# More warm-up matmuls ahead of the first products, and an early silu on ScalarE, in a two-layer adaptive FFN kernel

## The chip, the cores and the metric

The kernel runs on one core of a Trainium2 chip. The metric is the device time of one execution in microseconds; lower is better. A core has a matrix engine (TensorE, PE in the profile, with its weight loads shown as PEld), a vector engine (VectorE, DVE), a scalar engine (ScalarE, ACT), GpSimd (POOL) and SyncE (SP), which here issues DMA transfers. Each engine works through its own queue in order and waits on semaphores of the others.

## The reference

For x of 8 x 128 tokens with 512 features, two layers are computed, each as x + FFN(condition(x)).

```python
# layer 0
base = x @ W.T
logits = x @ Wr.T + 5.0 * one_hot(language_id)         # 8 experts
gates = softmax over the two largest logits, else 0
c = base + 2.0 * sum_e gates[e] * (x @ A[e].T) @ B[e].T  # rank 16
w_gu, w_d = dequant(4-bit weights, zeros, scales by group)
gate, up = split(c @ w_gu)                               # 1376 each
x = x + (silu(gate) * up) @ w_d
# layer 1
c = x @ weight[adapter_id].T                             # one of 8 per sequence
n = c * rsqrt(mean(c**2) + 1e-5) * ln_w
x = x + (silu(n @ gate_w.T) * (n @ up_w.T)) @ down_w.T   # 1792 inner
```

## The kernel before, in words

All activations lie transposed, features on the 128 partitions and tokens on the free axis, in two blocks of 512 tokens (`TB`). A float32 product that must be precise is made of three products of split operands (high part, low part, difference), with a rescale of the sum in PSUM between them.

The part that the change touches is the beginning, `network_in` and in it `by_groups_of_scales`. From `written_order()` on, the order of instructions on TensorE, VectorE, ScalarE and GpSimd is the order of the program text.

- L362 loads the router and low-rank weights `wa`, the eight x blocks `xb` of 128 tokens (block 0 in two halves from ScalarE's queue, blocks 1 to 7 from SP's), then the base weights `wT` and `bT`. They arrive in that order.
- L386 to L389: a tile of ones is set by VectorE, and TensorE multiplies it by itself `NWARM` times into a PSUM tile named `idle`, which nobody reads.
- L854: a one-element Exp on ScalarE into `root`, a cell of the tile `line`.
- `experts` (L436): for each x block, four matmuls of 128 x 136 give the router logits and the low-rank rows; 64 in all.
- L502 to L526: ScalarE and VectorE split x and the base weights.
- `base_products` (L533) adds the products of the base; `rescale_base` (L547) rescales its sums on ScalarE between products of the parts; `gated` (L455 to L482) makes the gates, with an Exp at L468; `turned` (L553) transposes them; `low_rank` (L559) adds the low-rank part; `split_condition` (L824 on ScalarE, L825 on VectorE) splits the result into the tile `a`.
- `gate_up_pair` (products at L682, rescales at L313 and L315): two chunks of 128 gate and up columns at a time, for each of four groups of scales. A gate sum ends in a silu on ScalarE (L698, tile `sl`), an up sum in a product on VectorE (L701, tile `h`). The four PSUM pairs are reused by the next chunk pair in the same order, so its first gate product waits for the first silu, and its first up product for the first `h`.
- `down` (L732), then layer 1: adaptation (L1292), normalisation, gate and up products (L1480), down products (L1628), all in an order that a planner in the kernel writes out.

ScalarE keeps one table of functions loaded at a time. The program contains no instruction for that: the compiler puts one (ACT_TABLE_LOAD in the profile) ahead of an activation whose function the loaded table lacks.

Of the kernel before, what the change touches and what calls it, by code (L numbers as in the profile page):

```python
# [20 lines left out]
AF = mybir.ActivationFunctionType  # L21
# [4 lines left out]
NT = B * T  # L26
TB = 512
NTB = NT // TB
NWARM = 20
KC = D // P  # L30
E, R = 8, 16
LANG_BIAS = 5.0
# [189 lines left out]
def network_in(ctx, tc, a, out, by_groups, flag, again):  # L222
    nc = tc.nc
# [8 lines left out]
    def bank(name):  # L232
        return pair(name)[:, 0, :]
# [10 lines left out]
    root = line[:, :1]  # L244
# [142 lines left out]
    idle = bank("idle")[:, :P]  # L387
    for _ in range(NWARM):
        nc.tensor.matmul(idle, lhsT=ones, rhs=ones, start=True, stop=True)  # L389
# [8 lines left out]
    eps = const.tile([P, 1], F32, name="eps")  # L398
# [93 lines left out]
    def x_parts(tb, b=None):  # L492
        rows = slice(tb * TB, (tb + 1) * TB) if b is None else slice(b * T, (b + 1) * T)
        at = slice(0, TB) if b is None else slice((b * T) % TB, (b * T) % TB + T)
        return a3[0][:, :, rows], a3[1][:, :, rows], xd[tb][:, :, at]

    def rows(tb):
        return range(tb * (TB // T), (tb + 1) * (TB // T))
# [15 lines left out]
    def x_diff(tb):  # L514
        for b in rows(tb):
            hi, lo, di = x_parts(tb, b)
            nc.vector.tensor_tensor(di, hi.bitcast(F32), lo.bitcast(F32), ALU.subtract)
# [28 lines left out]
    def rescale_base(ps):  # L546
        nc.scalar.activation(ps, ps, AF.Copy, scale=HLSCALE)  # L547
# [48 lines left out]
    def by_groups_of_scales():  # L596
# [25 lines left out]
        def queue_zeros(j0, j1, name):  # L622
            w = CH0[j0]
            zq = gup.tile([P, 2 * KC, j1 - j0, w], U16, tag="zq", bufs=1, name="zq")
            for j in range(j0, j1):
                zqs[j] = zq[:, :, j - j0, :]
            for s in range(8):
                queue("dve", name, 0.1 + 0.06 * (j1 - j0), lambda s=s: zeros_gu(zq, qz, s, j0, j1))
# [258 lines left out]
        hg1 = gated(1, [kept[:, i].rearrange("p (b n) -> p b n", b=2) for i in range(2)])  # L887
        for ps in pairs1:
            rescale_base(ps)
        x_diff(1)  # L890
        queue_zeros(0, 4, "zeros")
        for j in range(4):
# [259 lines left out]
    if by_groups:  # L1152
        by_groups_of_scales()
    else:
        in_float32()
# [725 lines left out]
```

## Time and profile before

| | us |
|---|---|
| median of 3 runs (lowest, highest) | 415.1 (414.18, 416.61) |
| profiled execution, its own time | 415.66 |
| span of the profile, first to last instruction | 413.6 |
| PE busy | 405.8 |
| DVE busy | 368.1 |
| ACT busy | 304.2 |
| POOL busy | 29.7 |

Busy time is the sum of the stretches in which an engine had an instruction running. A row of the timeline gives the start, the time from that start to the last instruction's end, the engine, the line, the operation with output and input tiles, the shape, the number of instructions merged, and in brackets the idle time ahead of it with the one that ended it. A row of the wait list gives who waited, for whom, the total in us, how many times, and the longest.

Four ACT_TABLE_LOAD instructions stand in the profile: at L854, L698, L807 and L1407, of 1.28 us each.

### The profile page before, as it was taken

Reading aid. Unit: us, or ns where it says so; the run is one execution under the profiler, and the core shown is the slowest. Engines: PE = TensorE matmul, PEld = TensorE weight load, DVE = VectorE, ACT = ScalarE, POOL = GpSimd, SP = SyncE. Lnnn points to the kernel's source line nnn. Section 1 sums busy time; section 2 is a strip of 40 time slices with the busy share of each in tenths; the row PEclk is TensorE's granted clock in tenths of the full one; section 3 lists DMA queues with packets and bytes.
Section 4 is the critical chain, followed back from the end, with each engine's and each line's share of the span. In section 5 each row is a group of like instructions: output and inputs, shape, how many; then the busy total and the mean of one; then the engine's idle time right before and its main releaser. Section 6 shows DMA issues by size and latency. Waiting matters only on the chain.

```text
span 413.6 us, 5170 instructions
## 1 busy us (share of the span) xinstructions
PE 405.8 (98%) x1763; PEld 319.1 (77%) x1763; DVE 368.1 (89%) x678; ACT 304.2 (74%) x501; POOL 29.7 (7%) x35
## 2 busy tenths in 40 slices
PE   8999999999999999999999999999999999999995
PEld 8886778888888867445777888888888888888884
DVE  3998979997999788988999999989999899988973
ACT  5832688867986887387999888866976688767751
POOL 1000200000000400421011011011011101000000
PEclk9999999999999999999999999999999999999999
DMA  8930840110020450682144114323333225000005
GB/s 280 397 148 0 241 91 0 52 26 32 2 63 2 151 180 1 215 309 73 52 141 89 65 25 119 84 52 91 101 65 90 71 45 140 0 1 2 25 2 208
DMA packets 17041, 38.59 MB, mean 93 GB/s; under 512 B 1904, under 2 KB 8944, under 8 KB 15984
## 3 DMA queue, kind: packets, MB, share of 16 engines
q1 hardware_dynamic: 11472, 25.09, 18.6%
q0 software_dynamic: 5104, 12.72, 12.2%
q10 hardware_dynamic: 432, 0.39, 0.3%
q8 instruction: 15, 0.25, 0.3%
q14 instruction: 18, 0.15, 0.1%
HBM read 36.10 MB, written 2.10 MB: 92 GB/s over the span
## 4 chain that ended last, share of the span: by engine, by line
PE 89%; DVE 5%; ACT 2%; DMA 1%; issue 1%; SPq 0%; ACTq 0%; DVEq 0%
PE bank L1480 30%; PE bank L1628 18%; PE down L732 9%; PE gate L682 9%; PE up L682 8%; PE bank L1292 6%; PE base L533 5%; PE experts L436 2%; PE base L559 2%; DMA xb<-in_first 1%; DVE xt L1260 1%; DVE a L1257 1%; PE bank L1333 1%; DVE down L315 1%; ACT sl L698 1%
## 5 line engine op out<-in xcount | busy, mean ns | idle before, releaser
L1227 ACT ACTIVATE bank<-bank 128x512 f32<-128x512 f32 (+1 forms) x126 | 71.2, 581 | 23.5 <-PE bank L1480 14.0
L1628 PE MATMUL bank<-h,d 128*128 128x512 f32 (+1 forms) x249 | 67.3, 382 | 0.0
L1628 PEld LDWEIGHTS bank<-h,d 128*128 128x128 f32 x249 | 45.6, 188 | 9.2 <-DVE h L1105 0.2
L682 PE MATMUL gate<-a,dq 128*128 128x512 f32 (+1 forms) x176 | 47.9, 394 | 0.4 <-ACT sl L698 0.4
L682 PE MATMUL up<-a,dq 128*128 128x512 f32 (+1 forms) x176 | 47.5, 392 | 0.0
L1480 PE MATMUL bank<-a,w 128*128 128x512 f32 x168 | 45.2, 391 | 0.4 <-ACT snap L1227 0.4
L1480 PE MATMUL bank<-xs,w 128*128 128x512 f32 x168 | 44.3, 391 | 0.0
L732 PE MATMUL down<-h,wd 128*128 128x512 f32 (+1 forms) x176 | 41.7, 391 | 0.1
L682 PEld LDWEIGHTS gate<-a,dq 128*128 128x128 f32 (+1 forms) x176 | 32.4, 185 | 9.0 <-ACT sl L698 0.9
L732 PEld LDWEIGHTS down<-h,wd 128*128 128x128 f32 (+1 forms) x176 | 32.9, 188 | 7.9 <-DVE h L701 0.5
L682 PEld LDWEIGHTS up<-a,dq 128*128 128x128 f32 (+1 forms) x176 | 32.3, 185 | 8.0 <-DVE a L825 0.3
L1480 PEld LDWEIGHTS bank<-a,w 128*128 128x128 f32 x168 | 31.2, 188 | 7.8 <-ACT snap L1227 0.8
L313 ACT ACTIVATE gate<-gate,ratio 128x1024 f32<-128x1024 f32 (+1 forms) x26 | 28.2, 1085 | 11.6 <-PE gate L682 11.6
L1480 PEld LDWEIGHTS bank<-xs,w 128*128 128x128 f32 x168 | 31.4, 188 | 6.5
L1227 ACT ACTIVATE snap<-bank 128x512 f32<-128x512 f32 x42 | 25.0, 596 | 13.6 <-PE bank L1480 13.4
L1108 DVE SCALAR_TENSOR_TENSOR w<-w 128x512 fp32r<-128x512 f32 x50 | 34.1, 682 | 0.1
L1095 POOL DMA_DIRECT2D raw<-in_wgu x14 | 17.9, 1281 | 199.0 <-PE up L682 46.2
L1685 DVE SCALAR_TENSOR_TENSOR xT<-bank,xT 128x512 f32<-128x512 f32 (+1 forms) x41 | 27.4, 673 | 4.2 <-PE bank L1628 3.8
L1514 DVE SCALAR_TENSOR_TENSOR snap<-bank,snap 128x512 f32<-128x512 f32 x42 | 28.2, 684 | 2.2 <-PE bank L1480 2.0
L1628 PE MATMUL bank<-w,d 128*128 128x512 f32 x96 | 30.0, 389 | 0.0
L1292 PE MATMUL bank<-w,xT 128*128 128x512 f32 x64 | 28.9, 594 | 0.0
L1105 DVE TENSOR_TENSOR w<-raw,w 128x512 fp32r<-128x512 f32 x42 | 28.6, 682 | 0.2 <-ACT w L1102 0.2
(169 smaller groups left out, 740.0 us busy)
## 6 DMA issues: line engine op xcount, KB each, us to landing
raw<-in_wgu SPq DMA_DIRECT2D x13, 640.0 KB, 3.9
raw<-in_wgu POOLq DMA_DIRECT2D x14, 256.0 KB, 4.5
wd<-in_wd SPq DMA_DIRECT2D x14, 256.0 KB, 2.6
qw<-in_qw_gu SPq DMA_DIRECT2D x5, 512.0 KB, 5.2
xT<-in_xT SPq DMA_DIRECT2D x2, 1024.0 KB, 12.0
xb<-in_first SPq DMA_DIRECT2D x7, 256.0 KB, 4.9
out<-xT SPq DMA_DIRECT2D x5, 256.0 KB, 2.2
qwd<-in_qw_d SPq DMA_DIRECT2D x2, 512.0 KB, 9.0
```

Source lines behind the costliest of these rows:

```text
L313: nc.scalar.activation(ps, ps, AF.Copy, scale=by)
L533: nc.tensor.matmul(base[m], lhsT=wT3[i][:, m, c * P : (c + 1) * P], rhs=x_parts(tb)[i][:, c, :], start=(i == 0 and c == 0), stop=(i == 1 a ...
L682: nc.tensor.matmul(ps, lhsT=dqs[j][:, c, half, :], rhs=a3[i][:, c, tb * TB : (tb + 1) * TB], start=(c == 0 and i == 0), stop=(i == 1), ski ...
L732: nc.tensor.matmul(ps[:, tb], lhsT=wds[k][:n, m * P : (m + 1) * P], rhs=h2[k][i][:, tb], start=(first and i == 0), stop=(i == 1), skip_gro ...
L1105: nc.vector.tensor_tensor(lo, raw, hi.bitcast(F32), ALU.subtract)
L1108: nc.vector.scalar_tensor_tensor(di, lo.bitcast(F32), -1.0 / EPS, hi.bitcast(F32), ALU.mult, ALU.add)
L1227: nc.scalar.activation(out_, in_, AF.Copy, scale=by)
L1292: nc.tensor.matmul(of("bank", "ad", b), lhsT=xT[:, c, b * T : (b + 1) * T], rhs=of("w1", b)[:, c * D : (c + 1) * D], start=(c == 0), stop= ...
L1480: nc.tensor.matmul(ps, lhsT=w[:, i, n, c * P : (c + 1) * P], rhs=x[i][:, c0 + c], start=(first and i == which[0] and c == 0), stop=True, s ...
L1514: nc.vector.scalar_tensor_tensor(x, of("bank", j, bank_), by, x, ALU.mult, ALU.add)
L1628: nc.tensor.matmul(of("bank", *who)[:, : c1 - c0], lhsT=of("d", j)[:, i, m * P : (m + 1) * P], rhs=h_tile(j, tb)[:, i, c0:c1], start=((i, ...
L1685: nc.vector.scalar_tensor_tensor(x, ps, by_end, x, ALU.mult, ALU.add)
```

## The change

The number of warm-up matmuls on the tile of ones goes from 20 to 33. Behind the rescales of the second token block's base sums, ScalarE runs a one-element silu of `eps` into `root`, the cell that L854 and L807 also write. No other instruction is edited, added or moved by hand.

```diff
-NWARM = 20
+NWARM = 33
...
         for ps in pairs1:
             rescale_base(ps)
+        nc.scalar.activation(root, eps, AF.Silu)
         x_diff(1)
```

## The prediction

> **What bounds the kernel now.** I read the page first, for who is busy and which chain ends last.
>
> ```profile
> span 413.6 us, 5170 instructions
> PE 405.8 (98%) x1763; PEld 319.1 (77%) x1763; DVE 368.1 (89%) x678; ACT 304.2 (74%) x501; POOL 29.7 (7%) x35
> PE 89%; DVE 5%; ACT 2%; DMA 1%; issue 1%; SPq 0%; ACTq 0%; DVEq 0%
> ```
>
> TensorE is busy for 98% of the span and is 89% of the chain. Nearly every microsecond that it loses or wins is therefore carried to the end, and I need the few places where it isn't doing useful work at full pace. The list of what it waited for, TensorE alone, longest in total first:
>
> ```profile
> PE idle L389 <- DVE ones L386: 1.1, 1, 1.1
> PE gate L682 <- ACT sl L698: 0.4, 1, 0.4
> PE experts L436 <- DMA xb<-in_first: 0.4, 2, 0.2
> ```
>
> The second and third are what this change touches. Now the order of time, TensorE alone, in the first 13 us, from four windows: the start of the span, a pair of narrow ones in the second x block, and one late in the experts.
>
> ```profile
> 1.06 2.32 PE L389 MATMUL idle<-ones 128*128 128x128 bf16 x20 [1.06 <-DVE ones L386]
> 3.60 2.18 PE L436 MATMUL experts<-wa,xb 128*128 128x136 f32 x8 [0.23 <-DMA xb<-in_first]
> 5.95 7.52 PE L436 MATMUL experts<-wa,xb 128*128 128x136 f32 x56 [0.17 <-DMA xb<-in_first]
> 13.22 3.99 PE L533 MATMUL base<-a,wT 128*128 128x512 f32 x16
> ...
> 6.57 0.66 PE L436 MATMUL experts<-wa,xb 128*128 128x136 f32 x2
> 6.34 1.34 PE L436 MATMUL experts<-wa,xb 128*128 128x136 f32 x5
> 8.79 4.33 PE L436 MATMUL experts<-wa,xb 128*128 128x136 f32 x36
> ```
>
> Matmuls of a row overlap, so I take their spacing. Five of the same matmul take 0.68 us more than two, so early they stand (1.34 - 0.66) / 3 = 0.227 us apart. Late, 36 take 4.33 us, of which the last one's own 0.28 us is taken off: 4.05 / 35 = 0.116 us. The pace doubles somewhere between 7.2 us and 8.8 us. The column of the granted clock prints 1.00 throughout these windows, so the clock is read here from the pace. The twenty warm-ups stand (2.32 - 0.31) / 19 = 0.106 us apart (one lasts 0.31 us).
>
> Last, the end of the first gate/up pair, all engines, where ScalarE loads its table for silu:
>
> ```profile
> 55.12 1.08 ACT L313 ACTIVATE up<-up,ratio 128x1024 f32<-128x1024 f32 x1
> 56.22 1.28 ACT L698 ACT_TABLE_LOAD   x1
> 57.16 1.07 PE L682 MATMUL up<-a,dq 128*128 128x512 f32 x4
> 57.51 2.12 ACT L698 ACTIVATE sl<-gate,small 128x1024 f32<-128x1024 f32 x2
> 58.66 2.48 DVE L701 SCALAR_TENSOR_TENSOR h<-up,small,sl 128x1024 f32<-128x1024 f32 x2 [2.66 <-ACT sl L698]
> 58.68 1.20 PE L682 MATMUL gate<-a,dq 128*128 128x512 f32 x4 [0.45 <-ACT sl L698]
> 59.72 1.16 PE L682 MATMUL up<-a,dq 128*128 128x512 f32 x4
> ```
>
> ScalarE is ready at 56.20; the load takes until 57.50, the first silu ends near 58.63, and only then is the gate bank free for TensorE's next pair.
>
> **Part A: 33 warm-ups.** It adds 13 matmuls on TensorE at 0.106 us: 1.38 us at the slow pace. Behind them in TensorE's queue stands everything else. Cover: the twentieth is followed by a hole from 1.06 + 20 x 0.106 = 3.18 to 3.60 us (x block 0 is on its way), and block 0 by another to 5.95 us (block 1). With 33 the first expert starts at 1.06 + 33 x 0.106 = 4.56, and eight of them end at 4.56 + 8 x 0.227 = 6.38, against block 1's landing at 5.95. If the faster pace comes no sooner than now, the cost is 0.43 us at most; the restart that vanishes gives some back (the first matmul of block 1 stands 6.34 - 5.95 = 0.39 us before the second, where 0.227 is usual: 0.16), which leaves 0.27. That is one end.
>
> The other end: the faster pace is there before 5.95. Then the 56 matmuls take 56 x 0.116 = 6.50 us in place of 13.22 - 5.95 = 7.27, a gain of 0.77. It can't be more for this execution, since the landing at 5.95 stays.
>
> Which? The pace doubled some 3.9 us after TensorE started on experts at 3.60, through one hole of about 0.37 us, though warm-ups had run for 2.1 us before the hole at 3.18. If a stream without the first hole earns the pace in the same 3.9 us, 33 warm-ups earn it at 1.06 + 3.9 = 4.96, ahead of 5.95. So I stand near the gain: -0.6, a fifth less than the full 0.77 because a single execution can't show how much the moment varies.
>
> [...]
>
> Does the gain last? Other work stays in time: ScalarE's first weight split waits for wT at 10.53, and the base products would need it at 13.22 - 0.77 = 12.45; it ends at 11.16. From there to 58 us the wait list shows TensorE waiting for nobody, so it carries the gain along.
>
> **Part B: the silu behind the rescales.** It adds a table load (1.28 us in all four loads of the trace) and a 128x1 ACTIVATE (0.20 us at L854): 1.48 us on ScalarE, and takes the load out of L698. ScalarE there, alone:
>
> ```profile
> 28.93 1.01 ACT L547 ACTIVATE base<-base 128x1024 f32<-128x1024 f32 x1 [0.86 <-PE base L533]
> 34.29 1.02 ACT L824 ACTIVATE a<-base 128x1024 fp32r<-128x1024 f32 x1 [4.35 <-PE base L559]
> ```
>
> The next instruction, the split at L824, waits 4.35 us for TensorE. The added 1.48 us lies inside with 2.87 to spare: cost nothing. Without that cover it would delay the split by up to 1.48. The last Exp (L468, 25.80) is ahead, and what follows up to L698 are copies, which run between the silus of L698 today without a load. The added ACTIVATE writes a cell of its own and adds no DMA and no wait but for the memset of eps, done at 1.2 us.
>
> At L698 the first silu would then run from 56.22 to 57.34 and the second to 58.46. TensorE's groups of four stand 0.91 us apart, so it reaches the next gate group at 57.16 + 0.91 = 58.07, finds the bank free, and wins 58.68 - 58.07 = 0.61. The two groups after the stall, 1.20 and 1.16 us against 1.07, would lose their slow starts: 0.13 + 0.09 = 0.22 more. What is late next: the up bank, freed by VectorE's h, which moves to about 57.36-58.60, and TensorE wants it at 58.98. Second bank, second h: 59.84 against 60.79. So nothing takes the wait's place by these rows. Bounds: 0.45 (the hole alone) and 0.83; I take 0.7, between the two that count spacing.
>
> [...]
>
> **Sum.** The profiled execution took 415.66 us, its span plus 2.0 around it. -0.6 - 0.7 = -1.3 gives 414.4. It lay 0.56 over the median, 415.1; from the median the same sum gives 413.8, a change of -0.31%. I forecast that. About 0.5%, 2.1 us, is what a measurement of this kernel can tell from no change, and the three runs span 2.4 us.
>
> **Rivals.**
> 1. *The pace comes no sooner; only the table load pays.* For it: I infer the release from one execution. Then +0.27 - 0.7 = -0.4: 414.7 us.
> 2. *Before usually does worse than its profile.* A release later by 1 us costs 1 - 0.116/0.227 = 0.49 us, and if the hole at 5.58-5.95 also spoils the count in many executions, release would come 3.9 us after 5.95, at 9.85, some 2.3 us later: 1.1 us that the change would save as well. For it: runs that differ by 2.4 us. Against: the median is below the profile, not above. -0.77 - 0.83 - 1.1 = -2.7: 412.4 us.
> 3. *Slower: the warm-ups hold back x.* Mechanism: 33 end at 4.56, after block 0 (3.60), and the slow pace lasts. If block 1 lands soon after block 0 there is no second hole, and the whole 0.96 us is lost. It decides once the release stays past 7.5 us and the table load's gain is under 0.3, for instance because VectorE's queue, 89% busy, takes the stall over. Then +0.96: 416.1. Against it: block 1 landed 2.35 us after block 0, and VectorE idled 2.66 us ahead of h.
> 4. *Nothing reaches the end*: later waits, such as those at L1480 (0.7 us in all), absorb it: 415.1. They hang on ScalarE and VectorE, which also run earlier, so I give this little.
>
> **How the numbers follow.** Forecast (both gains, -0.7 to -1.6): 0.60. Rival 1: 0.16; rival 2: 0.13; rival 3: 0.06; rival 4: 0.05. The forecast's own range is 413.5 to 414.4 by the terms; a median of runs that span 2.4 us may move by some 0.8 us, which gives 412.7 and 415.2. I widen to 412.6 to 415.2, which takes in rivals 1 and 4. Faster by over 0.5% needs under 413.0: most of rival 2 and a tenth of the forecast with spread and rival 1: 0.20. Slower by over 0.5% needs over 417.2, beyond rival 3 without spread: 0.04. Within: 0.76.
>
> **What would show it.** After: 33 matmuls at L389 ending near 4.6 us; no wait before the first expert; the pace of 0.116 us by block 1; base products from about 12.5 us. The table load on the new line near 29 to 30 us, three others, none at L698; the wait of gate L682 for sl gone from TensorE's list. A is wrong if experts after 6 us still stand 0.227 apart in most executions; B is wrong if another releaser stands in front of the gate or up groups at about 58 us.

## The result and the profile after

The changed kernel takes 418.74 us (median of 6 runs, 418.37 to 419.05) against 414.87 us for the kernel before. The ratio is 1.0087, with a 95% interval from 1.0073 to 1.0100: slower by 0.9%, outside the predicted range and on the other side of no change. Its profiled execution took 419.05 us with a span of 417.1, 3.5 more than before.

The list of what TensorE waited for, kernel after (who, for whom, total us, times, longest), is where to look first:

```profile
PE bank L1293 <- DVE xT L744: 2.4, 1, 2.4
PE idle L389 <- DVE ones L386: 1.1, 1, 1.1
PE bank L1481 <- ACT snap L1228: 0.4, 1, 0.4
```

Both waits that the change aimed at are gone, the one of L682 for silu and the one of the experts for x. A new one has come: the first adaptation product of layer 1 (L1293 now, L1292 before, because the change adds a line) waits 2.4 us for VectorE's last write of xT (L744). It lies some 135 us after the added silu has run.

The order of time on TensorE, kernel after, at the three places:

```profile
1.06 3.70 PE L389 MATMUL idle<-ones 128*128 128x128 bf16 x33 [1.06 <-DVE ones L386]
4.56 8.86 PE L436 MATMUL experts<-wa,xb 128*128 128x136 f32 x64
13.17 0.71 PE L533 MATMUL base<-a,wT 128*128 128x512 f32 x2
...
58.02 1.07 PE L682 MATMUL gate<-a,dq 128*128 128x512 f32 x4
58.93 1.07 PE L682 MATMUL up<-a,dq 128*128 128x512 f32 x4
...
166.93 8.83 PE L1293 MATMUL bank<-w,xT 128*128 128x512 f32 x16 [2.36 <-DVE xT L744]
175.60 0.60 PE L1334 MATMUL bank<-ident,nx 128*128 128x128 f32 x4
```

And the same last place in the kernel before:

```profile
165.33 7.03 PE L1292 MATMUL bank<-w,xT 128*128 128x512 f32 x16
172.20 0.60 PE L1333 MATMUL bank<-ident,nx 128*128 128x128 f32 x4
```

Read the starts against those of before. The base products begin at 13.17 and not at 13.22: -0.05. The gate products behind the first silu begin at 58.02 and not at 58.68, without the slow restarts; the long stretch of down products at L732 stands at 155.57 for 156.47, so layer 0 nears its end 0.90 us ahead. The adaptation begins at 166.93 for 165.33, 1.60 behind: 2.50 us were lost in between. Its first 16 matmuls then take 175.60 - 166.93 = 8.67 us where they took 172.20 - 165.33 = 6.87: 1.80 more. -0.90 + 2.50 + 1.80 = +3.40, of the span's 3.5.

The 1.80 us has its own view, the windows of TensorE in the kernel after (stretch, its length, busy us and count, the granted clock, then the DMA share and GB/s):

```profile
164.50:166.90 2.40, 0.08 (x1) 1.00 0.18 24
167.50:170.90 3.40, 3.40 (x6) 0.50 0.64 267
170.90:175.00 4.10, 4.10 (x11) 1.00 0.19 40
```

The idle stretch is followed by 3.4 us at half the clock. In the kernel before the same middle stretch is:

```profile
167.50:170.90 3.40, 3.40 (x9) 1.00 0.86 308
```

**Where the wait comes from.** VectorE isn't late: its five writes of xT start at 161.90 in the kernel after (first row) and at 162.81 before (second), and last 4.98 and 4.99 us.

```profile
161.90 4.98 DVE L744 SCALAR_TENSOR_TENSOR xT<-down,small,xT 128x1024 f32<-128x1024 f32 x5 [1.08 <-PE down L732]
162.81 4.99 DVE L744 SCALAR_TENSOR_TENSOR xT<-down,small,xT 128x1024 f32<-128x1024 f32 x5 [1.09 <-PE down L732]
```

TensorE started in the middle of them before, and behind the last of them after. The program shows why. Layer 1 takes the eight PSUM banks in the hand-written order `FREED = [2, 3, 6, 7, 0, 1, 4, 5]`; the first adaptation product writes bank 2. Layer 0's PSUM pairs are handed out by the layer under the kernel when the program is built, not by the kernel's text, and the two built programs differ there from the second gate/up pair on (a pair is two banks of one sum; m counts the four blocks of output features, in the order in which VectorE reads them):

| PSUM pair (first of two banks) | before | after |
|---|---|---|
| first gate, up, gate, up | 0, 2, 4, 6 | 0, 2, 4, 6 |
| second gate, up, gate, up | 0, 4, 2, 6 | 0, 2, 4, 6 |
| last down sums, m = 0, 1, 2, 3 | 2, 6, 0, 4 | 4, 6, 0, 2 |

`FREED` fits the left column: bank 2 holds the down sum of m = 0, which VectorE reads first. In the right column bank 2 holds m = 3, read last. The order of the products in TensorE's queue is the same in both from the first expert to the end of layer 1; only this placement and the semaphores that go with it differ.

### The profile page after: what moved, and what is told of

Read it like the earlier page. It is cut to its first block, busy times and chain, and to the rows that moved or that the text cites. A ratio compares the mean times of both kernels' runs of the same rounds, so it can differ in the third digit from the quotient of the medians.

```text
span 417.1 us, 5196 instructions
## 1 busy us (share of the span) xinstructions
PE 407.8 (98%) x1776; PEld 320.7 (77%) x1776; DVE 368.3 (88%) x678; ACT 304.6 (73%) x502; POOL 27.1 (6%) x35
## 4 chain that ended last, share of the span: by engine, by line
PE 90%; DVE 6%; ACT 2%; issue 1%; DVEq 0%
PE bank L1481 30%; PE bank L1629 18%; PE gate L682 9%; PE up L682 9%; PE down L732 8%; PE bank L1293 6%; PE base L533 5%; PE experts L436 2%; PE base L559 2%; PE idle L389 1%; DVE xT L744 1%; DVE xt L1261 1%; DVE a L1258 1%; PE bank L1334 1%; DVE down L315 1%
## 5 line engine op out<-in xcount | busy, mean ns | idle before, releaser
L682 PE MATMUL gate<-a,dq 128*128 128x512 f32 (+1 forms) x176 | 47.7, 393 | 0.0
L682 PE MATMUL up<-a,dq 128*128 128x512 f32 (+1 forms) x176 | 47.4, 391 | 0.0
L732 PE MATMUL down<-h,wd 128*128 128x512 f32 (+1 forms) x176 | 41.7, 391 | 0.1
L732 PEld LDWEIGHTS down<-h,wd 128*128 128x128 f32 (+1 forms) x176 | 32.9, 188 | 7.9 <-DVE h L701 0.5
L682 PEld LDWEIGHTS gate<-a,dq 128*128 128x128 f32 (+1 forms) x176 | 32.5, 185 | 8.2 <-ACT gate L313 0.6
L682 PEld LDWEIGHTS up<-a,dq 128*128 128x128 f32 (+1 forms) x176 | 32.4, 185 | 7.8 <-DVE a L825 0.3
L1293 PE MATMUL bank<-w,xT 128*128 128x512 f32 x64 | 30.7, 625 | 2.4 <-DVE xT L744 2.4
```

Source lines behind the costliest of these rows:

```text
L682: nc.tensor.matmul(ps, lhsT=dqs[j][:, c, half, :], rhs=a3[i][:, c, tb * TB : (tb + 1) * TB], start=(c == 0 and i == 0), stop=(i == 1), ski ...
L732: nc.tensor.matmul(ps[:, tb], lhsT=wds[k][:n, m * P : (m + 1) * P], rhs=h2[k][i][:, tb], start=(first and i == 0), stop=(i == 1), skip_gro ...
L1293: nc.tensor.matmul(of("bank", "ad", b), lhsT=xT[:, c, b * T : (b + 1) * T], rhs=of("w1", b)[:, c * D : (c + 1) * D], start=(c == 0), stop= ...
```

## The experiments

My theory at this point: the silu alone changes the hand-out of PSUM, `FREED` no longer fits, the first adaptation product waits for the last bank, and the idle stretch then halves the clock. The main rival: the warm-ups, which shift all of TensorE's work in time, bring the half clock on, and alone they are about as slow as the whole change. The first four kernels ran on one chip, with the kernel before at 415.22 us (25 runs).

**The warm-ups alone.**

```diff
-NWARM = 20
+NWARM = 33
```

> Only the 33 warm-ups, without the silu. Theory (the silu made the compiler's layer hand out the PSUM pairs in another order, so that bank 2, which the first adaptation product takes, is the last to come free): no loss here; 414.2 to 414.9, clock 1.000, no wait of the adaptation for xT. [...]

Measured: 414.80 us, ratio 0.9984 (0.9969 to 0.9999). The wait list has no xT in it, and the wait for silu is back:

```profile
PE idle L389 <- DVE ones L386: 1.1, 1, 1.1
PE gate L682 <- ACT sl L698: 0.4, 1, 0.4
PE bank L1480 <- ACT snap L1227: 0.4, 1, 0.4
```

The program built from this kernel hands out PSUM as in the left column of the table. The warm-ups are not the cause; they gain a little.

**The silu alone.**

```diff
         for ps in pairs1:
             rescale_base(ps)
+        nc.scalar.activation(root, eps, AF.Silu)
```

> Only the silu, 20 warm-ups. Theory: all of the loss; TensorE waits some 2.4 us for the last xT at the first adaptation product and a stretch of half clock of 3.4 us follows; 418.2 to 419.2. [...]

Measured: 418.85 us, ratio 1.0071 (1.0044 to 1.0099). TensorE's row at the wait, and its window behind it:

```profile
165.63 8.83 PE L1293 MATMUL bank<-w,xT 128*128 128x512 f32 x16 [2.36 <-DVE xT L744]
```

```profile
166.00:169.40 3.40, 3.40 (x5) 0.50 0.75 296
```

The same wait, to the hundredth, and the same half clock; the program built from this kernel has the right column of the table. The whole loss is the silu's. One of the six runs, at 417.34 us, had a mean granted clock of 0.999, the other five 0.995 to 0.996.

**The whole change with a list that fits the new placement.**

```diff
-FREED = [2, 3, 6, 7, 0, 1, 4, 5]
+FREED = [4, 5, 6, 7, 0, 1, 2, 3]
```

> The whole change, and the list FREED, by which layer 1 takes the PSUM banks, goes from 2,3,6,7,0,1,4,5 to 4,5,6,7,0,1,2,3, so that the first adaptation product takes the bank that comes free first. Theory: the wait of 2.4 us and the half clock are gone, and the early gains are left: 0.8 from the silu and 0.1 to 0.7 from the warm-ups, 413.4 to 414.1. [...]

Measured: 414.04 us (413.54 to 414.85, 12 runs), ratio 0.9965 (0.9948 to 0.9982). TensorE goes from the down products into the adaptation without a stop, at full clock:

```profile
159.73 3.79 PE L732 MATMUL down<-h,wd 96*128 96x512 f32 x16
163.37 4.03 PE L1293 MATMUL bank<-w,xT 128*128 128x512 f32 x9
```

```profile
163.30:167.30 4.00, 4.00 (x11) 1.00 0.37 106
```

Both edits stay, and eight numbers turn the ratio from 1.0087 into 0.9965. This version is also faster than the kernel before, by 0.35%.

**The kernel before with the list that doesn't fit it.** The same diff of `FREED`, on the kernel before.

> The kernel before with only FREED changed to 4,5,6,7,0,1,2,3, so that the first adaptation product takes the bank of the last down sum. Theory: the loss without either edit: a wait of some 2.4 us for xT and 1.7 us of half clock, 418.8 to 419.6. Rival (table load or warm-ups needed): 415, as before.

Measured: 419.57 us (8 runs, 417.02 to 421.71), ratio 1.0079 (1.0051 to 1.0108). Neither edit is in it, and the loss is:

```profile
169.33 4.97 PE L1292 MATMUL bank<-w,xT 128*128 128x512 f32 x7 [2.36 <-DVE xT L744]
```

```profile
169.80:173.80 4.00, 4.00 (x7) 0.57 0.55 229
```

The mismatch by itself is enough. The eight runs fall into two groups that the mean granted clock tells apart: three at 0.999 took 417.02 to 417.76 us, five at 0.988 to 0.996 took 419.34 to 421.71. 3.4 us at half the clock take 0.004 off the mean of such a span, so 0.999 leaves no room for them: with the wait alone, the kernel takes 417.0 to 417.8 us. That is the first hint that the half clock comes in some executions only and is worth some 2 us of the total. A hint only: the mean also falls by other stretches, and in the profiled run, the slowest of the eight, the base products began late too (below).

**The wait without the half clock.** Extra matmuls on the identity, into bank 4, which is free early, keep TensorE at work while bank 2 is awaited.

```diff
             def adapt(_, c=c):
+                if i == 0 and c == 0 and by_groups:
+                    for _ in range(NFILL):
+                        nc.tensor.matmul(bank_tiles[4][:, :P], lhsT=ident, rhs=ident, start=True, stop=True)
```

With `NFILL = 20`:

> The changed kernel with 20 extra float32 matmuls of 128x128 on the identity, into bank 4 (free early), ahead of the first adaptation product: they do nothing but keep TensorE at work during the wait for bank 2. Theory (2.4 us of wait, and 1.8 us of half clock that the idle stretch brings on): the wait stays, the half clock goes, 416.7 to 417.2. Rival (the half clock comes from something else, or the wait is longer by itself): no better than the change, 418.5 to 419.

Measured: 418.83 us, ratio 1.0085 (1.0066 to 1.0104), a miss. The order of time shows that it was the experiment's size:

```profile
164.01 4.63 PE L1296 MATMUL bank<-ident 128*128 128x128 f32 x40
168.47 7.03 PE L1297 MATMUL bank<-w,xT 128*128 128x512 f32 x16
161.49 4.98 DVE L745 SCALAR_TENSOR_TENSOR xT<-down,small,xT 128x1024 f32<-128x1024 f32 x5 [1.11 <-PE down L733]
```

Twenty float32 matmuls show as 40 records and hold the first product back to 168.47, while the last xT was written by 161.49 + 4.98 = 166.47 us (third row): 2.0 us too long, about what the half clock costs. The half clock itself was gone (16 matmuls in 7.03 us, as before the change). So once more with `NFILL = 10`:

> As the run with 20 extra matmuls on the identity, but with 10: each takes two passes, 40 records and 4.5 us were seen with 20, so that they outlasted the wait by 2.0 us. With 10 they end at about 166.3 us, inside the wait for bank 2. Theory (wait of 2.4 us and 1.8 us of half clock): the wait is left, the half clock gone, 416.6 to 417.1. Rival (the loss is the wait alone and the half clock costs nothing at the end): 418.5 to 419, as with the change.

Measured: 417.27 us (416.60 to 417.51), against 414.74 for the kernel before, run beside it (9 runs); ratio 1.0056 (1.0042 to 1.0069), just below the change's 1.0073 to 1.0100. The median is 0.17 us above the range expected and 1.2 below the rival's.

```profile
164.38 2.40 PE L1296 MATMUL bank<-ident 128*128 128x128 f32 x20
166.90 7.13 PE L1297 MATMUL bank<-w,xT 128*128 128x512 f32 x16
173.87 0.60 PE L1338 MATMUL bank<-ident,nx 128*128 128x128 f32 x4
```

```profile
166.80:170.90 4.10, 4.00 (x10) 1.00 0.67 248
```

The wait is left, 166.90 - 164.38 = 2.52 us in this profile, now filled with work that nobody reads. The half clock is gone, and the difference of the ratios, 0.0031 x 415 = 1.3 us, goes with it; the ratios' intervals nearly touch, so its size is better read from the traces (16 matmuls in 8.67 us with it, in 166.90 to 173.87 = 6.97 without: 1.7).

**What each edit is worth without the mismatch.** The kernel before, run beside these two, was at 415.26 us (23 runs). First the silu with 20 warm-ups and the fitting list:

> Only the silu with 20 warm-ups, and FREED as 4,5,6,7,0,1,2,3. Theory (the table load at L698 cost TensorE 0.8 us): 0.8 below before, 414.2 to 414.5; against the same with 33 warm-ups it shows what those are worth. Rival (the early silu gains nothing where the median is taken): as before.

Measured: 414.32 us (413.51 to 415.92, 12 runs), ratio 0.9983 (0.9970 to 0.9996). Then the same with 24 warm-ups:

> Silu, FREED as 4,5,6,7,0,1,2,3, and 24 warm-ups, which end at about 3.6 us, when x block 0 lands: the hole ahead of the first expert is filled and no expert is held back. Theory (33 hold the experts back by 1 us and win that back only through an earlier full clock): the same as 33 within 0.3 us, 413.6 to 414.3. Rival (only a longer warm-up brings the clock sooner): as with 20, 414.3 or more.

Measured: 414.11 us (413.69 to 414.78, 12 runs), ratio 0.9966 (0.9951 to 0.9981), as good as 33 (0.9965). That points to the hole which both fill, and not to the number of warm-ups, as what counts; but the interval with 20 overlaps both, so it isn't shown. What shows is a narrower spread: the kernel before took 416.6 us or more in 9 of its 63 runs, while none of the 36 runs with 24 or 33 warm-ups and without the wait for bank 2 took over 415.63. (With the silu and a fitting list, twelve runs span 2.41 us with 20 warm-ups, most of it by one run at 415.92, 1.09 with 24 and 1.31 with 33.) The start of the base products in the profiles fits. With 20 they begin at 13.22, 11.85, 14.72 and 12.35 us (kernel before and the three experiments), with 24 at 12.42, with 33 at 13.17, 12.25, 12.12, 12.73 and 13.07. An execution in which block 1 of x came late shows the long case:

```profile
5.74 8.65 PE L436 MATMUL experts<-wa,xb 128*128 128x136 f32 x55 [1.06 <-DMA xb<-in_first]
```

It is the profile of the kernel before with the other list: a hole of 1.06 us, and base products only at 14.72.

## Why the prediction was wrong

**The step that failed** is in part B, "So nothing takes the wait's place by these rows". The rows that I meant were those of the next products, and I took it for granted that an edit of one ScalarE instruction leaves everything else in the program as it was, and priced only time. It changed where sums lie in PSUM, and another wait did come, at layer 1 instead of L682: 2.36 us for VectorE's last write of xT, with 3.4 us of half clock behind it. None of the four rivals had this in it: rival 3 lost time at the front, and rival 4 came nearest, with later waits that absorb the gain, but looked at the waits that stood in the list already. The slower side got 0.04.

The kernel's text had the warning, and I named neither half of it: `FREED` is a hand-written order of banks that holds only for one hand-out of PSUM, and the hand-out is not written anywhere. The text on the kernel before even says that the PSUM pairs are reused in the same order. That was wrong, and the profile before showed it: in its weight loads, the second pair's first up product is released by a silu, not by VectorE's h:

```profile
59.68 0.76 PEld L682 LDWEIGHTS up<-a,dq 128*128 128x128 f32 x4 [0.24 <-ACT sl L698]
```

An up sum that waits for a silu sits where a gate sum was. So part B's line that h frees the first up bank was wrong as well; there it cost nothing, since the second silu, forecast for 58.46, was early enough for 58.98.

**Part A** held in size, within its noise, but not in the rule that it was chosen by. Forecast -0.6; the changed kernel's profile shows -0.05, but over runs the warm-ups alone gain 0.42 us by medians (414.80 for 415.22) and 0.0016 x 415 = 0.7 by the ratio, whose interval reaches from 0.04 to 1.3 us. The rule was that an unbroken stream earns the full pace 3.9 us after it starts, at 4.96. In the packed traces the record of the granted clock begins where the experts' spacing halves from 0.227 to 0.116 us, at 7.56 us in the kernel before. With 33 warm-ups that moment lies at 7.06 (the changed kernel), 4.34, 4.93, 5.05 and 6.87, with 24 at 6.39, with 20 also at 5.58, 5.97 and 9.89. So 4.96 was one case of many: the five with 33 spread over 2.72 us, from 4.34 to 7.06. The bounds were -0.77 and +0.27; the base products of the five profiles with 33 moved by -0.05 to -1.10 against 13.22. Rival 2's late release, which is this moment and was put at 9.85, does occur, at 9.89 in the profile with the start at 14.72, one of four with 20 warm-ups.

**Part B** held in its mechanism. The load moved into ScalarE's idle stretch (row below), no load is left at L698, and TensorE gained 0.85 us there (-0.05 at the base products, -0.90 before the end of layer 0), a little over the 0.83 that I gave as the upper bound, for 0.7 taken. Over runs the silu with a fitting list gains 0.0017 x 415 = 0.7 us (0.9983).

```profile
29.86 1.28 ACT L890 ACT_TABLE_LOAD   x1
```

The added ACTIVATE starts at 31.16, 1.30 us behind the start of the load.

**The sum** was right for another kernel. With `FREED` fitted, the whole change measures 414.04 us where I forecast 413.8, and 0.9965 where I forecast 0.9969. Part of that agreement is luck, since part A's -0.6 came from a rule that didn't hold. The missing term was +2.5 us of wait and +1.8 us of half clock by the profiles, 4.3 us together; the ratios with and without the fitted list are 0.0122 x 415 = 5.1 us apart, and their intervals allow 3.8 to 6.3.

**The signs that I listed** were at the front and at L698. Those on the warm-ups, the table load and the wait for silu came true; the full pace by block 1 and base products at about 12.5 us did not in this profile, though they did in others. None of them looked at the rest of the kernel, where the loss was.

What stays open: why the layer that builds the program hands the second up sum a different pair once the silu is in. The table shows that it does, and the silu-only kernel that no other edit is needed.

## What to carry to other kernels

Before pricing an edit in time, ask which decisions of the build hang on it: buffer hand-out and semaphores can change far away from the edit, and a list written by hand to fit one hand-out (here the order of the banks) turns into a wait when it does. When TensorE is the bound, compare its wait list over the whole span, not at the edit, and look behind every new idle stretch, such as the 2.36 us here, for the half clock that may follow. A small gain can be real and still be buried: refit the hand-written order before judging the edit.

## What the runs showed of the hardware

An idle stretch of TensorE of 2.36 us was enough for 3.4 us of half clock in the changed kernel's profile, at a cost of 1.8 us. It was so in all three profiles with the unfilled wait (the changed kernel, the silu alone, the kernel before with the other list), each time with 2.36 us. It need not do it in every execution: one run of six with the silu alone and three of eight with the other list have a mean clock of 0.999, which has no room for it. For the runs without a profile a lower mean doesn't prove the half clock, because other stretches lower it too: the profile with the silu, 20 warm-ups and the fitting list has a mean of 0.996 and half clock only at its end, from 408.8 us on, where TensorE has nothing left to do.

The clock records of the traces place it alike: in all three profiles the half clock begins 160.43 us after the first entry of the record, which is 47.0 times its own length of 3.413 us, and that first entry lies anywhere from 4.34 to 9.89 us in the ten profiles. In each of the three the whole idle stretch lies inside the 3.413 us that end as the half clock begins; in the changed kernel these are 164.08 to 167.49, with TensorE idle from 164.57 to 166.93. No profile here has an idle stretch of that length between two products that lies otherwise, so what one would cost is not shown. Filling the gap with ten useless matmuls kept the clock at 1.00.
